# A two-layer graph network on one core: the first stage in another order, and one gather in eighty fetched row by row by SyncE

## The chip, the cores and the metric

The kernel runs on one core of a Trainium2 chip. The metric is the device time of one execution in microseconds (us). Nine runs of the kernel before gave a median of 4908.98 us (4884.85 to 4942.95).

## The reference, cut to what matters

12,500 nodes with 128 features, 200,000 edges sorted by their target `dst`. All numbers are float32.

```
h = relu(layernorm(x))
agg = segment_sum(h[src], dst)
x = x + agg @ W_rel.T + b_rel + h @ W_root.T          # layer 0

h = relu(layernorm(x))
ew = silu(edge_attr_50 @ We1 + be1) @ We2 + be2       # one row of 128 per edge
agg = segment_sum(h[src] * ew, dst)
x = x + h + (silu(agg @ Wn1 + bn1) @ Wn2 + bn2)       # layer 1
```

## The kernel before

**Tiles.** A tile is 128 edges, a group is 8 tiles (1024 edges); there are 196 groups in each layer, and the last has 3 tiles. Nodes are worked on in 25 batches of 512.

**One group.** `fetch` (L205) has GpSimd (POOL) issue one indirect DMA for each tile (L214): 128 rows of 128 floats are gathered from HBM into one of six buffers `hs`. The buffer of group k is free when the scatter of group k-6 is done (L208). `compare` (L223) builds on VectorE (DVE) a 0/1 matrix `oh` of 128 edges by a window of 128 targets for each tile. `scatter` (L328, matmul L336) multiplies the 8 gathered tiles with their `oh` on TensorE (PE) and sums them in one PSUM bank; `add` (L344, L353) adds that bank into `agg` in SBUF, at an offset that it loads into registers (L347).

**Layer 0** gathers rows of h. For the first 28 groups (FG = number of batches + FB, L110) h is not in HBM yet, so the raw x is gathered and normalised in SBUF by `norm` (L275), two half groups of 4 tiles each. Beside each of the first 25 groups `node_root` (L377) normalises one batch of nodes, stores h to HBM (`h0_d`), transposes it on PE (L396), copies the result on ScalarE (ACT, L405), and multiplies it with W_root after a matmul that lays the bias b_rel down (L407, L409); DVE then adds x and writes `keep` (L417). I call this stretch the first stage. `push` (L265) runs the first half of a unit at once and the second half with the next unit; `later` holds the steps after that. From group 28 on rows of `h0_d` are gathered, for which POOL waits until all batches are stored (L212). When all edges of a batch are summed, `node_sum`, `node_norm` and `node_keep` (L422 to L458) finish it: agg times W_rel (L429), layer norm, h stored to `h1_d` by SP.

**Layer 1** also has for each group g the edge weights. `hidden(g+2)` (L298) takes the edge features: for each pair of groups SP loads 400 KB into one of two buffers `ef` (`load`, L290, DMA L295; the buffer is free when `hidden` of the pair before the last is done, L294), PE multiplies with We1 (L306), ACT applies silu (L309). `weigh(g+1)` (L312) multiplies with We2 (L317); DVE adds the bias (L324) and multiplies the gathered rows in place (L326). When a batch is complete, `node_hidden` and `node_out` (L461, L470) compute its output, DVE adds `keep` (L483) and SP stores it (`out_x`, L370, after the wait at L485).

**Order.** Every engine works through its own instructions in the order in which the loop L590 to L615 emits them; a wait (`at`) holds all that stands behind it on that engine. Within one iteration g of layer 1 the order is: add(g-1), hidden(g+2), scatter(g), weigh(g+1), then the steps on nodes that `plan` (L568) put beside this group. So SP's list in layer 1 is made of `ef` loads, each two iterations ahead of its use, and of output stores, each of which waits for the newest result of DVE. A store falls into every eighth iteration or so: iterations 10, 18, 26, 34, 42, 50, then 59, 67, ... 139, then 146, 154, ... 186, and two at the end.

Of the kernel before, what the change touches and what calls it, by code (L numbers as in the profile page):

```python
# [11 lines left out]
I32 = mybir.dt.int32  # L12
# [6 lines left out]
P = 128  # L19
D = 128  # L20
# [7 lines left out]
OB = 3  # L28
EG = 2
XB = 4  # L30
FB = 3
EPS = 1e-5


# [31 lines left out]
    return need  # L66


@with_exitstack
def kernel(  # L70
    ctx: ExitStack,
# [1 line left out]
    n_edges: int,  # L73
    x: bass.AP,
    src_t: bass.AP,
    dst_t: bass.AP,
    ef_t: bass.AP,
    need: bass.AP,
# [42 lines left out]
    def single(shape, name, dtype=F32):  # L121
        return const.tile(shape, dtype, name=name)
# [3 lines left out]
    agg = single([P, NW * WG], "agg")  # L126
    keep = single([P, -(-N // P), D], "keep")
    src_sb = single([P, NT], "src_sb", I32)
    rel = single([P, NG, GT], "rel")
    base_i = single([1, NG], "base_i", I32)  # L130
    bad_i = single([1, 1], "bad_i", I32)
# [11 lines left out]
    with (  # L143
# [7 lines left out]
        inside_n, = many(1, [P, 1], "inside_n")  # L151
        total, = many(1, [1, 2], "total")
        hs = many(HB, [P, GT, D], "hs")
        oh = many(OB, [P, GT, W], "oh")
        ef = many(2, [P, EG * GE], "ef")
        dst_i = ef[1][:, :NT].bitcast(I32).rearrange("p (g t) -> p g t", t=GT)
# [48 lines left out]
        def fetch(layer, g):  # L205

            k = layer * NG + g
            at(G, done["src", 0 if g < 8 else 1], done.get(("ap", k - HB)))  # L208
            if layer:
                at(G, *(done["h1 out", b] for b in range(max(0, NBT - 2), NBT)))  # L210
            elif g >= FG:
                at(G, *(done["h0 out", b] for b in range(max(0, NBT - 3), NBT)))  # L212
            for t in range(tiles_of[g]):
                ins = G.indirect_dma_start(  # L214
                    out=hs[k % HB][:, t, :], out_offset=None,
                    in_=h1_d if layer else x if g < FG else h0_d,
                    in_offset=bass.IndirectOffsetOnAxis(
                        ap=src_sb[:, g * GT + t : g * GT + t + 1], axis=0
                    ),
                )  # L220
                done["hs", k] = inc(ins, f"hs{k % HB}", 16)

        def compare(layer, g):  # L223
            n = tiles_of[g]
# [87 lines left out]
        def weigh(g):  # L312

            n = tiles_of[g]
            at(T, done["hid", g], done.get(("msg", g - 1)), done["keep", NBT - 1])
            for t in range(n):
                ins = T.matmul(  # L317
                    wp[:, t, :], hid[g % 2][:, t * P : (t + 1) * P], we2_sb, start=True, stop=True
                )
            done["wp", g] = inc(ins, "pe")  # L320
            compare(1, g)
            at(V, done["wp", g])
            w, h = wp[:, :n, :], hs[(NG + g) % HB][:, :n, :]
            ins = V.tensor_add(w, w, be2_sb.unsqueeze(1).to_broadcast([P, n, D]))  # L324
            at(V, inc(ins, "dve"), done["hs", NG + g])
            done["msg", g] = inc(V.tensor_mul(h, w, h), "dve")  # L326

        def scatter(layer, g):  # L328
            k = layer * NG + g
            if layer:  # L330
                at(T, done["msg", g])
            else:
                at(T, done["h of", g] if g < FG else done["hs", k], done["oh", k])
            at(T, done.get(("add", k - AB)))
            for t in range(tiles_of[g]):
                ins = T.matmul(  # L336
                    ap[k % AB], hs[k % HB][:, t, :], oh[k % OB][:, t, :],
                    start=(t == 0), stop=(t == tiles_of[g] - 1),
                )
            done["ap", k] = inc(ins, "pe")  # L340

# [35 lines left out]
        def node_root(b):  # L377

            n0, nt = batches[b]
            xr, h, i = xt[b % XB], h0[b % 3], b % 2  # L380
            dev = []

            def first():
                dev.append(
                    stats(xr, nt, P, stn[i], mvn[i], sdn[i], (done["xt", b], done.get(("h0", b - 2))))
                )

            def second():
                at(A, scales(nt, P, mvn[i], sdn[i], rsn[i], nmn[i], *dev))
                at(A, done.get(("h0 out", b - 3)), done.get(("tp", b - 3)))  # L390
                done["h0", b] = normalized(h, xr, nt, P, rsn[i], nmn[i])
                at(S, done["h0", b])
                done["h0 out", b] = node_dma(b, h, h0_d, f"h0out{b % 3}", False)
                at(T, done["h0", b], done.get(("hT", b - 1)), done["ident"])
                for t in range(nt):
                    ins = T.transpose(tp[:, t, :], h[:, t, :], ident)  # L396
                done["tp", b] = inc(ins, "pe")
                later.append((clock[0] + 1, lambda: node_root_b(b)))

            return first, second  # L400

        def node_root_b(b):
            n0, nt = batches[b]
            at(A, done["tp", b], done.get(("rp", b - 1)))
            done["hT", b] = inc(A.copy(hT[0][:, :nt, :], tp[:, :nt, :]), "act")  # L405
            at(T, done["hT", b], done.get(("kept", b - 1)), done["const"], done["ones"])
            T.matmul(rp[:, :nt, :], ones_r, b_rel_r[:, :nt, :], start=True, stop=False)  # L407
            for t in range(nt):
                ins = T.matmul(rp[:, t, :], hT[0][:, t, :], w_root_sb, start=False, stop=(t == nt - 1))  # L409
            done["rp", b] = inc(ins, "pe")  # L410
            later.append((clock[0] + 1, lambda: node_root_c(b)))

        def node_root_c(b):
            n0, nt = batches[b]
            t0 = n0 // P
            at(V, done["rp", b])
            ins = V.tensor_add(keep[:, t0 : t0 + nt, :], rp[:, :nt, :], xt[b % XB][:, :nt, :])  # L417
            done["kept", b] = inc(ins, "dve")
            if b + XB < NBT:
                node_load(b + XB)  # L420

        def node_sum(b):  # L422

            n0, nt = batches[b]
            t0 = n0 // P
            at(T, done["add", ready[b]], done.get(("keep", b - 1)), done["const"])
            for t in range(nt):
                s = n0 + t * P
                ins = T.matmul(op[:, t, :], agg[:, s : s + P], w_rel_sb, start=True, stop=True)  # L429
            done["op", b] = inc(ins, "pe")  # L430
            at(V, done["op", b], done["kept", b])
            o = op[:, :nt, :]
            ins = V.tensor_add(o, o, keep[:, t0 : t0 + nt, :])  # L433
            done["dev", b] = stats(
                op, nt, P, stn[2], mvn[2], sdn[2], (inc(ins, "dve"), done.get(("h1", b - 1)))
            )
            ins = V.memset(agg[:, n0 : n0 + nt * P], 0.0)
            done["agg"] = inc(ins, "dve")
# [51 lines left out]
        with tc.tile_critical():  # L490
# [8 lines left out]
            for b in range(min(XB, NBT)):  # L499
                node_load(b)  # L500
            done["need"] = inc(S.dma_start(out=need_f, in_=need), "need", 16)
            for t, ap_ in (
                (w_root_sb, w_root_t), (b_rel_r, b_rel.unsqueeze(1).to_broadcast([1, NB, D])),
                (w_rel_sb, w_rel_t), (we1_sb, we1), (we2_sb, we2),
                (wn1_sb, wn1), (wn2_sb, wn2), (be1_sb, be1), (bn1_sb, bn1),
                (be2_sb, be2.to_broadcast([P, D])),
                (bn2_r, bn2.unsqueeze(1).to_broadcast([1, NB, D])),
            ):
                done["const"] = inc(S.dma_start(out=t, in_=ap_), "const", 16)
# [74 lines left out]
            for layer in range(2):  # L584
# [5 lines left out]
                for g in range(NG):  # L590
# [2 lines left out]
                        fetch(layer, g + 1)  # L593
                    if not layer:
                        if g + 1 < NG:
                            ins = compare(0, g + 1)
                        if g:
                            done["oh", k + 1] = add(0, g - 1)
                        elif g + 1 < NG:
                            done["oh", k + 1] = inc(ins, "dve")  # L600
                        if g < FG:
                            for c in range(-(-tiles_of[g] // NB)):
                                push(norm(g, c))
                            push(node_root(g) if g < NBT else nothing)
                        scatter(0, g)
                    else:
                        if g:
                            add(1, g - 1)
                        if g + 2 < NG:
                            hidden(g + 2)  # L610
                        scatter(1, g)
                        if g + 1 < NG:
                            weigh(g + 1)
                    for what in beside[layer].get(g, ()):
                        what()  # L615
                add(layer, NG - 1)
                for what in beside[layer].get(NG, ()):
                    what()
# [184 lines left out]
```

## Time and profile before

The profiled execution took 4917.91 us; its span, from the first to the last instruction, is 4916.0 us. It is 8.9 us above the median of the nine runs.

| stretch (us from the start) | what runs | POOL busy | PE busy | DVE busy | granted PE clock |
|---|---|---|---|---|---|
| 0 to 418 | layer 0, groups 0 to 27 (rows of x) | 236.74 | 213.37 | 173.73 | 0.65 |
| 418 to 2320 | layer 0, the other 168 groups | 1254.14 | 539.90 | 322.70 | 0.61 |
| 2320 to 4916 | layer 1, 196 groups | 1468.00 | 1465.10 | 756.29 | 0.74 |

How to read it: one indirect DMA of POOL is shown as 0.95 us (946 ns in the mean) and the next starts 0.30 us later when POOL waits for nothing, so a gather takes 1.25 us and a group of eight 10.0 us. The 0.30 us is not counted as busy. Groups in the table's stretches take (418 to 2320) 1902/168 = 11.3 us and (2320 to 4916) 2596/196 = 13.2 us each. In the lists below a row of the timeline is: start in us, length in us, engine and line, operation, written tile <- read tiles, count, and in brackets the idle time of the engine before it and what ended it. In a view of waits the columns are total us, times, longest us. "remote" and "another core or an unknown queue" stand for a wait whose end the profile can't attribute; "issue" for time in which the engine waited for nothing that the profile shows. SPq is SP issuing a DMA, not the transfer.

### The profile page before, as it was taken

How to read it: one execution, taken by the hardware profiler on the slowest of the kernel's cores; microseconds unless marked ns; L12 is line 12 of the kernel's file. 1: busy time of each engine (PE TensorE's matmuls, PEld its weight loads, DVE VectorE, ACT ScalarE, POOL GpSimd, SP SyncE). 2: the span in 40 equal slices, each digit the busy share in tenths (PEclk: the TensorE clock that was granted, in tenths of full speed). 3: DMA queues.
4: the chain of work that ended last, by engine and by line, in shares of the span. 5: the costliest groups of instructions: out<-in, count | busy, mean ns of one | idle time of the engine just before them, and what ended most of it. 6: DMA issues, size and time to landing. Idle time of an engine off the chain costs nothing.

```text
span 4916.0 us, 30563 instructions
## 1 busy us (share of the span) xinstructions
PE 2218.4 (45%) x11000; PEld 1786.3 (36%) x11000; DVE 1252.7 (25%) x2369; ACT 453.4 (9%) x778; POOL 2958.9 (60%) x3133
## 2 busy tenths in 40 slices
PE   3662332222322323224466556455445555556666
PEld 2442322222222223223344444343333343444444
DVE  2442211111111111112223233232222222333333
ACT  3441000000000000000001001010000000000101
POOL 6556666666666666665666566555544555566663
PEclk6666555655666666566677777777677777777777
DMA  3321211111111111112222222122222122222221
GB/s 85 82 71 47 54 48 50 50 48 50 49 49 50 49 48 52 49 49 55 59 58 66 58 63 63 52 54 54 52 57 53 52 55 54 57 58 60 70 66 43
DMA packets 159390, 274.89 MB, mean 56 GB/s; under 512 B 53231, under 2 KB 104058, under 8 KB 154330
## 3 DMA queue, kind: packets, MB, share of 16 engines
q0 software_dynamic: 100032, 205.07, 16.1%
q1 hardware_dynamic: 59002, 67.70, 5.0%
q8 instruction: 89, 1.46, 0.1%
q14 instruction: 71, 0.58, 0.0%
q10 hardware_dynamic: 196, 0.09, 0.0%
HBM read 253.44 MB, written 19.20 MB: 55 GB/s over the span
## 4 chain that ended last, share of the span: by engine, by line
another core or an unknown queue 45%; PE 23%; issue 15%; DVE 11%; DMA 2%; ACT 1%; DVEq 1%; POOL 0%; SPq 0%; POOLq 0%
PE bank L336 12%; PE pair L317 4%; DVE pair L324 3%; PE pair L306 3%; DVE oh L227 2%; DMA ef<-in_ef_t 2%; DVE hs L326 2%; DVE agg L353 1%; DVEq L347 1%; ACT h L257 1%; PE pair L407 1%; PE pair L409 1%; DVE st L238 1%; DVE stn L238 0%
## 5 line engine op out<-in xcount | busy, mean ns | idle before, releaser
L214 POOL DMA_INDIRECT hs<-h_d,src_sb x2902 | 2745.7, 946 | 1768.0 <-issue 838.0
L336 PE MATMUL bank<-oh,hs 128*128 128x128 f32 x6252 | 1164.2, 362 | 1893.5 <-issue 658.4
L336 PEld LDWEIGHTS bank<-oh,hs 128*128 128x128 f32 x6252 | 1088.9, 270 | 2093.4 <-issue 1385.4
L324 DVE TENSOR_TENSOR pair<-pair,be_sb 128x1024 f32<-128x1024 f32 x196 | 240.9, 1229 | 1746.2 <-remote 1029.5
L306 PE MATMUL pair<-ef,we_sb 50*128 50x512 f32 (+1 forms) x782 | 423.2, 661 | 283.9 <-DMA ef<-in_ef_t 251.6
L227 DVE TENSOR_TENSOR oh<-bank,rel 128x1024 f32<-128x1024 f32 x392 | 474.5, 1211 | 0.1
L317 PE MATMUL pair<-we_sb,hid 128*128 128x128 f32 x3126 | 443.3, 301 | 13.7 <-issue 6.7
L353 DVE TENSOR_TENSOR agg<-agg,bank 128x128 f32 x392 | 110.9, 283 | 1324.2 <-remote 1094.2
L317 PEld LDWEIGHTS pair<-we_sb,hid 128*128 128x128 f32 x3126 | 434.1, 221 | 13.2 <-issue 9.5
L309 ACT ACTIVATE hid<-pair,be_sb 128x1024 f32<-128x1024 f32 x196 | 217.8, 1111 | 2210.7 <-remote 1007.3
L306 PEld LDWEIGHTS pair<-ef,we_sb 50*128 50x128 f32 x782 | 139.6, 198 | 434.0 <-DMA ef<-in_ef_t 256.3
L214 POOL DMA_INDIRECT hs<-in_x,src_sb x224 | 212.0, 946 | 137.9 <-PE bank L336 66.4
L326 DVE TENSOR_TENSOR hs<-pair,hs 128x1024 f32<-128x1024 f32 x196 | 239.3, 1221 | 15.5 <-DMA hs<-h_d,src_sb 8.8
L429 PE MATMUL bank<-w_rel_sb,agg 128*128 128x128 f32 x196 | 45.7, 397 | 316.2 <-issue 200.4
L243 ACT ACTIVATE sdn<-mvn,eps 128x4 f32<-128x4 f32 (+1 forms) x50 | 14.8, 297 | 1764.4 <-DVE mvn L241 1384.8
L429 PEld LDWEIGHTS bank<-w_rel_sb,agg 128*128 128x128 f32 x196 | 39.4, 294 | 320.0 <-issue 202.7
L433 DVE TENSOR_TENSOR bank<-bank,keep 128x512 f32<-128x512 f32 (+1 forms) x25 | 17.2, 689 | 321.0 <-remote 248.8
L257 ACT ACTIVATE hs<-hs,nm,rs 128x128 f32<-128x128 f32 x224 | 91.5, 480 | 10.7 <-DVE nm L250 6.4
L396 PE MATMUL pair<-ident,h 128*128 128x128 f32 x98 | 26.1, 417 | 113.1 <-ACT h L257 82.4
L407 PE MATMUL pair<-b_rel_r,ones_r 1*128 1x512 f32 (+1 forms) x50 | 50.9, 1119 | 35.8 <-issue 29.4
L396 PEld LDWEIGHTS pair<-ident,h 128*128 128x128 f32 x98 | 16.3, 204 | 119.3 <-ACT h L257 88.0
L409 PEld LDWEIGHTS pair<-w_root_sb,hT 128*128 128x128 f32 x196 | 43.7, 327 | 36.8 <-issue 36.8
(57 smaller groups left out, 565.9 us busy)
## 6 DMA issues: line engine op xcount, KB each, us to landing
hs<-h_d,src_sb POOLq DMA_INDIRECT x2902
ef<-in_ef_t SPq DMA_DIRECT2D x98, 400.0 KB
h_d<-h SPq DMA_DIRECT2D x48, 256.0 KB
xt<-in_x SPq DMA_DIRECT2D x24, 256.0 KB
out_x<-xt SPq DMA_DIRECT2D x24, 256.0 KB
hs<-in_x,src_sb POOLq DMA_INDIRECT x224
ef<-in_dst_t SPq DMA_DIRECT2D x1, 784.0 KB, 4.5
src_sb<-in_src_t SPq DMA_DIRECT2D x1, 752.0 KB, 6.0
```

What stands on the lines that cost most here:

```text
L214: ins = G.indirect_dma_start(out=hs[k % HB][:, t, :], out_offset=None, in_=h1_d if layer else x if g < FG else h0_d, in_offset=bass.Indire ...
L227: return V.tensor_tensor(oh[k % OB][:, :n, :], io.unsqueeze(1).to_broadcast([P, n, W]), rel[:, g, :n].unsqueeze(2).to_broadcast([P, n, W]) ...
L257: ins = A.activation(h[:rows, t, :], xr[:rows, t, :], AF.Relu, bias=nm_[:rows, t : t + 1], scale=rs_[:rows, t : t + 1],)
L306: ins = T.matmul(hp_b[:, c : c + m], we1_sb, e[:, c : c + m], start=True, stop=True)
L309: ins = A.activation(hid[g % 2][:, :n], hp_b[:, :n], AF.Silu, bias=be1_sb)
L317: ins = T.matmul(wp[:, t, :], hid[g % 2][:, t * P : (t + 1) * P], we2_sb, start=True, stop=True)
L324: ins = V.tensor_add(w, w, be2_sb.unsqueeze(1).to_broadcast([P, n, D]))
L326: done["msg", g] = inc(V.tensor_mul(h, w, h), "dve")
L336: ins = T.matmul(ap[k % AB], hs[k % HB][:, t, :], oh[k % OB][:, t, :], start=(t == 0), stop=(t == tiles_of[g] - 1),)
L353: done["add", k] = inc(V.tensor_add(window, window, ap[k % AB]), "dve")
L407: T.matmul(rp[:, :nt, :], ones_r, b_rel_r[:, :nt, :], start=True, stop=False)
L409: ins = T.matmul(rp[:, t, :], hT[0][:, t, :], w_root_sb, start=False, stop=(t == nt - 1))
```

## The change

It has three parts.

1. In the first stage `compare` and the normalising units come before `add`, which moves to just ahead of `scatter`; `node_root` is cut into four steps instead of three, with two units between transpose and copy and two between the root matmuls and `keep`. The bias matmul of b_rel leaves this stage and goes into `node_sum`, ahead of its wait for `add`.
2. FB goes from 3 to 4, so that 29 groups are gathered from x.
3. For 35 groups (16 in layer 0: 40, 50, ... 190; 19 in layer 1: 11, 21, ... 191) POOL gathers only the first 7 tiles. The rows of the eighth are fetched by SP, one DMA of 512 bytes for each row, into a buffer `hx` (two of them). `rows(layer, g)` is emitted at the end of every iteration, behind the steps on nodes: it loads 12 or 16 of the 128 row numbers from SBUF into SP's registers in one instruction, and then issues one register instruction and one DMA for each row. Ten iterations fill one tile, which is used two iterations later. In all these are 4480 row DMAs, and SP's list grows by some 9,300 instructions. `scatter` waits for `hx` ahead of its last tile, and in layer 1 DVE multiplies the last tile apart.

```diff
-FB = 3
+FB = 4
+RG = 10
...
+def rows_apart(n_nodes, n_edges):
+    full = n_edges // GE
+    tiles = []
+    for layer in range(2):
+        begin = 0 if layer else -(-n_nodes // (NB * P)) + FB
+        while begin + RG + 1 < full:
+            tiles.append((layer, begin + RG + 1, begin))
+            begin += RG
+    return tiles
...
-            for t in range(tiles_of[g]):
+            for t in range(tiles_of[g] - ((layer, g) in place)):
                 ins = G.indirect_dma_start(
...
+        def rows(layer, g):
+            for i, (l, at_g, begin) in enumerate(apart):
+                if l != layer or not begin <= g < begin + RG:
+                    continue
+                lo, hi = (P // 4 * (g - begin + j) // RG * 4 for j in range(2))
+                if g == begin:
+                    at(S, done["rows"], done["ap", apart[i - 2][0] * NG + apart[i - 2][1]] if i > 1 else None)
...
+                _, nodes = nc.values_load_multi_w_load_instructions(
+                    row_sb[i : i + 1, lo:hi], engines=[mybir.EngineType.SP], min_val=0, max_val=N - 1,
...
+                for p, node in zip(range(lo, hi), nodes):
+                    ins = S.dma_start(
+                        out=hx[i % 2][p : p + 1, :], in_=(h1_d if layer else h0_d)[ds(node, 1), :]
+                    )
+                    done["hx", i] = inc(ins, f"hx{i % 4}", 16)
...
-            done["msg", g] = inc(V.tensor_mul(h, w, h), "dve")
+            i = place.get((1, g))
+            if i is not None:
+                V.tensor_mul(h[:, : n - 1, :], w[:, : n - 1, :], h[:, : n - 1, :])
+                at(V, done["hx", i])
+                ins = V.tensor_mul(hx[i % 2], w[:, n - 1, :], hx[i % 2])
...
-                later.append((clock[0] + 1, lambda: node_root_b(b)))
+                later.append((clock[0] + 2, lambda: node_root_b(b)))
...
-            T.matmul(rp[:, :nt, :], ones_r, b_rel_r[:, :nt, :], start=True, stop=False)
             for t in range(nt):
-                ins = T.matmul(rp[:, t, :], hT[0][:, t, :], w_root_sb, start=False, stop=(t == nt - 1))
+                ins = T.matmul(rp[:, t, :], hT[0][:, t, :], w_root_sb, start=True, stop=True)
             done["rp", b] = inc(ins, "pe")
-            later.append((clock[0] + 1, lambda: node_root_c(b)))
-
-        def node_root_c(b):
+            later.append((clock[0] + 2, lambda: node_root_d(b)))
...
-            at(T, done["add", ready[b]], done.get(("keep", b - 1)), done["const"])
+            at(T, done.get(("keep", b - 1)), done["const"], done["ones"])
+            T.matmul(op[:, :nt, :], ones_r, b_rel_r[:, :nt, :], start=True, stop=False)
+            at(T, done["add", ready[b]])
...
                         if g + 1 < NG:
-                            ins = compare(0, g + 1)
-                        if g:
-                            done["oh", k + 1] = add(0, g - 1)
-                        elif g + 1 < NG:
-                            done["oh", k + 1] = inc(ins, "dve")
+                            compared = compare(0, g + 1)
+                            if not g:
+                                done["oh", 1] = inc(compared, "dve")
                         if g < FG:
                             for c in range(-(-tiles_of[g] // NB)):
                                 push(norm(g, c))
                             push(node_root(g) if g < NBT else nothing)
+                        if g:
+                            done["oh", k + 1] = add(0, g - 1)
                         scatter(0, g)
...
                     for what in beside[layer].get(g, ()):
                         what()
+                    rows(layer, g)
```

## The prediction

> **What bounds the kernel now.** I read in this order: busy shares, costliest groups, waits by stage, then the timeline around one output store in layer 1, and SP's rows of issue durations. From the page's costliest groups:
>
> ```profile
> L214 POOL DMA_INDIRECT hs<-h_d,src_sb x2902 | 2745.7, 946 | 1768.0 <-issue 838.0
> L306 PE MATMUL pair<-ef,we_sb 50*128 50x512 f32 (+1 forms) x782 | 423.2, 661 | 283.9 <-DMA ef<-in_ef_t 251.6
> ```
>
> A gather is 946 ns, and most of POOL's "issue" idle is 0.30 us between two gathers: 1.25 us each, 10.0 us a group. Layer 0 after the first stage takes 1902/168 = 11.3 us a group, so POOL is nearly the bound there. Layer 1 takes 13.2: something else holds POOL for some 3 us a group. The waits of layer 1 (2320 to 4916) say what:
>
> ```profile
> POOL hs L214 <- PE bank L336: 541.1, 74, 18.3
> PE pair L306 <- DMA ef<-in_ef_t: 250.1, 22, 21.1
> ```
>
> POOL waits for scatters (its buffers are all full), and PE's `hidden` waits 22 times, 11.4 us each, for an `ef` load. There are 22 to 24 output stores. The timeline at one of them:
>
> ```profile
> 3111.33 0.68 DVE L483 TENSOR_TENSOR xt<-bank,keep 128x512 f32<-128x512 f32 x1
> 3112.04 0.41 SPq L370 DMA_DIRECT2D out_x<-xt  x1
> 3112.49 0.86 SPq L295 DMA_DIRECT2D ef<-in_ef_t  x2
> ...
> 3117.55 3.78 PE L306 MATMUL pair<-ef,we_sb 50*128 50x512 f32 x4 [19.12 <-DMA ef<-in_ef_t]
> 3121.26 3.78 PE L336 MATMUL bank<-oh,hs 128*128 128x128 f32 x16
> ...
> 3125.31 0.94 POOL L214 DMA_INDIRECT hs<-h_d,src_sb  x1 [17.96 <-PE bank L336]
> ```
>
> The reader sees a chain: the store waits on DVE, the `ef` load stands behind the store in SP's list, PE waits for the load, the scatter stands behind `hidden` on PE, POOL waits for the scatter. From store to `hidden` it is 5.5 us; at the other stores I read it is 5.1 to 7.1. At this point nothing covers a later `ef` load: its delay is paid in full.
>
> The first stage has its own pace. Gathers of successive groups start at 147.85, 160.72, 173.97, 187.27: 13.2 us a group. Its waits (100 to 350):
>
> ```profile
> DVE keep L417 <- PE pair L409: 87.2, 17, 5.1
> POOL hs L214 <- PE bank L336: 61.8, 19, 3.6
> ```
>
> DVE stands 5.1 us at L417 for the root matmuls of that same iteration, compares and adds stand behind it, and POOL waits some 3 us a group. At its end:
>
> ```profile
> 387.12 0.95 POOL L214 DMA_INDIRECT hs<-h_d,src_sb  x1 [34.99 <-DMA h_d<-h]
> ```
>
> **First stage in the other order.** `keep` now comes two units after the root matmuls, the copy two after the transpose, and the bias matmul (2.07 us a batch, L407) no longer stands ahead of the scatter. That removes the 5.1 us wait. What is late next is POOL itself: I take layer 0's pace, 11.3, for some 21 groups: 21 × (13.2 − 11.3) = −40. The 35 us wait is for the last h store; the batches end earlier by the same pace but POOL arrives earlier too, and the 29th group from x adds 11 us of work ahead of it; I take −15. Together **−55**. Ends: 0 (DVE's and ACT's lists are as long as before, so another wait may replace this one), and −102 (21 × the 3.2 us above the gathers' 10.0, and all 35). The bias matmul in `node_sum` is ahead of that step's wait for `add`; PE idles 316.2 us ahead of L429 in 25 batches, so it costs nothing; uncovered it would be 25 × 1.2 = 30.
>
> **One gather less in 35 groups.** 35 × 1.25 = **−44**; the end is 0, where POOL was not last. DVE's split multiply in layer 1 is one more instruction of about 0.28 us (L353 takes 283 ns for 128x128), and the larger one shrinks by about 0.13: 19 × 0.15 = **+3**.
>
> **Rows by SP.** 128 rows a tile, over ten iterations: ten loads of registers, 128 register instructions, 128 DMA issues, all on SP's queue. The trace has no one-row DMA from an address in a register on SP. The nearest rows (min/median/max ns, then first and last start):
>
> ```profile
> L295 SPq DMA_DIRECT2D ef<-in_ef_t x98: 281/282/462, 2244.5 to 4856.3; - x98
> L370 SPq DMA_DIRECT2D h_d<-h x51: 332/365/421, 48.1 to 2303.6; - x51
> L509 SPq DMA_DIRECT2D b_rel_r<-in_b_rel x1: 736/736/736, 8.2 to 8.2; - x1
> L501 SPq DMA_DIRECT2D need_f<-in_need x1: 2056/2056/2056, 5.6 to 5.6; - x1
> L347 DVEq FUSED_REGOPS  x392: 183/186/206, 23.5 to 4891.2; - x196
> L347 DVEq TENSOR_LOAD <-base_i x98: 339/343/602, 22.9 to 4889.9; - x98
> ```
>
> The register instruction is 0.186 on DVE's queue, with gaps of some 0.04 to 0.05 around it. The DMA is bounded below by 0.28 (50 rows) and above by 2.06 (one row, need_f, right behind four large loads at the start); b_rel_r, four rows, took 0.74. Most issues, and all those in steady running, are 0.28 to 0.41, so I take 0.37: 0.19 + 0.04 + 0.37 + 0.05 = **0.65 us a row**. Ends 0.33 (issue and gap alone) and 2.3. The load of 12 or 16 values I take at 0.40, near the 0.34 of four values (up to 4 × 0.34 = 1.37). A tile is 128 × 0.65 + 10 × 0.4 = 87 us of SP; ten groups are 113 us in layer 0 and 132 in layer 1. So SP keeps up, `hx` is there in time, and the waits for it cost 0. SP becomes the bound above 0.85 us a row in layer 0, and 1.0 in layer 1.
>
> The Trainium skill speaks against the 0.37 ("DMA: Bandwidth & Descriptors", "Why a DMA increments its semaphore by 16 and not by 1"): a transfer of fewer than 16 pieces uses fewer engines, and the issuing sequencer itself writes the semaphore increments of the engines not used. A one-row DMA would thus have 15 of them; the rows of 0.74 (four) and 2.06 (one) beside 0.28 fit that order. The page has no time for it; by 2.06 the sum would be the last rival's. The same page ("Latency and other measured facts") puts a `tensor_load` at 600 ns at least; this trace shows 343, and by 600 the 35 loads priced below would add 9 us.
>
> **What stands behind the rows.** `rows(g)` is at the end of every iteration, so whatever SP issues next stands behind it: in layer 0 the h stores and in layer 1 the output stores and the `ef` loads. In layer 0 the store of h1 has slack. In layer 1 an `ef` load without a store ahead of it is issued two iterations before its use, and 8 to 9 us of rows per group fit into that. But after an output store, which waits for DVE far along in the group, the rows now stand between the store and the `ef` load that PE waits for. From SP's list in the changed kernel: 12 stores in even iterations (10 to 50 and 146 to 186) have 24 to 28 rows and two loads of registers ahead of the next `ef` load, 304 rows and 24 loads in all; 11 stores in odd ones (59 to 139) have 12 to 16 rows and one load: 144 rows and 11 loads. So 448 × 0.65 + 35 × 0.40 = 291 + 14 = **+305**. Low end: 448 × 0.33 + 35 × 0.34 = 160; and 0, if something covers it. What could cover it is an `ef` buffer ahead or PE working on something else; the timeline shows PE idle 19 us at that point, and POOL out of buffers.
>
> **Sum.** −55 − 44 + 3 + 305 = +209. On the profiled execution's own 4917.9 that is 5127; this execution lies 8.9 above the median, so against the runs' median 5118, rounded to **5120**.
>
> **Rivals.**
>
> *Gains fail, stalls come.* First stage and gathers give nothing (an engine other than POOL is last in both): 4909 + 308 = 5217. For it: "remote" waits in the trace show that other engines progress poorly while POOL issues in long bursts (in layer 1, `DVE pair L324 <- remote: 1029.5, 89, 16.7`). I count it within the forecast's own range, 5020 to 5240, with it **0.50**.
>
> *Half the stall is taken up* (POOL refills its six buffers, and the pair after a store runs at 10 us a group where the mean is 13.2): 4909 − 96 + 155 = 4968; 4935 to 5020, **0.12**.
>
> *Faster.* One mechanism: the `ef` load is not late. The place is SP's list behind the 23 output stores; the price is 448 rows, against a gain of 96 − 5 = 91 us. It decides when a row costs under 91/448 = 0.2 us there, or when the wait for the store moves so that PE reaches `hidden` later than the load anyway. Then 4909 − 91 = 4818. Against it: even an issue alone has not been under 0.28, and PE waits for `ef` in 22 of 23 cases. For it: the register instruction could run beside the issue. **0.17**.
>
> *No change.* Stalls of some 90 us eat the gains exactly; 4885 to 4935, about 4910, **0.08**.
>
> *SP becomes the bound.* The one-row issue costs 0.74, so a row 0.74 + 0.19 + 0.09 = 1.02, a tile 132 to 135 us: layer 0 then loses 16 × (132 − 113) = +304, `ef` 448 × 1.02 + 14 = +471, gains −95: about 5590. At 2.3 us a row 4480 × 2.3 alone is over 10,000. For it: the two smallest transfers have the longest issues. Against it: both stood at the start behind other issues. **0.13**.
>
> **How the numbers follow.** About 0.5% (25 us) is what a measurement of this kernel can tell. Slower by more: 0.50 + 0.12 + 0.13 = 0.75. Faster 0.17, same 0.08. The range goes from the faster case's 4820 to 5420, leaving out most of SP as the bound and half of the faster case: 4820 to 5420. The likeliest case alone is 5020 to 5240.
>
> **What the profile after would show.** The row DMAs on SP near 0.37 us; from output store to `hidden` some 14 us (odd stores) and 22 us (even ones) instead of 5.5; PE waiting for `ef` some 550 us in all instead of 250, and POOL's waits for L336 up by about the same; the first stage at some 11.3 us a group and the 35 us wait shorter; no wait of PE for `hx`. It would be wrong if a row costs over 0.85 us (waits for `hx` on PE and DVE), or if waits for `ef` don't grow, or if the first stage keeps 13 us.

## The result and the profile after

The changed kernel took 5640.53 us (median of 10 runs, 5618.43 to 5660.88), the kernel before beside it 4912.02 (31 runs): ratio 1.1481, interval 1.1452 to 1.1509. The profiled execution took 5631.3 us, its span is 5629.4. Ratios leave out runs far above the others of their kernel: one in experiment 4 (6941.4 us) and one in experiment 5 (4858.81 us).

That holds on one kind of chip. The experiments fell on several chips, and these are of two kinds: on some the kernel before takes 4862 to 4961 us, on others 3996 to 4004, and there the changed kernel is faster, 3895.67 us, ratio 0.9746 (0.9729 to 0.9762). I call them the first and the second kind. The prediction and the result above are of the first kind. A ratio is always to the kernel before on the same chip.

**Where the 713 us of the two profiled executions lie** (5631.3 − 4917.9), by the starts of gathers that open a stretch:

| stretch | before | after | difference |
|---|---|---|---|
| to the first gather of group 29 | 397.13 | 354.27 | −42.9 |
| from there to the first gather of layer 1 (2306.34; 2732.71) | 1909.2 | 2378.4 | +469.2 |
| from there to the end | 2611.6 | 2898.6 | +287.0 |

The chain that ended last, in the kernel before and then in after, and from the page of after its costliest groups (busy us, mean ns | idle before, and what ended most of it):

```profile
another core or an unknown queue 45%; PE 23%; issue 15%; DVE 11%; DMA 2%; ACT 1%; DVEq 1%; POOL 0%; SPq 0%; POOLq 0%
```
```profile
SPq 28%; issue 26%; another core or an unknown queue 19%; PE 16%; DVE 8%; DMA 2%; ACT 1%; DVEq 0%; POOL 0%
...
L231 POOL DMA_INDIRECT hs<-h_d,src_sb x2859 | 2705.8, 946 | 2536.7 <-PE bank L388 1286.4
...
L347 PE MATMUL pair<-ef,we_sb 50*128 50x512 f32 (+1 forms) x782 | 435.6, 681 | 569.0 <-DMA ef<-in_ef_t 567.8
...
L388 PE MATMUL bank<-oh,hx 128*128 128x128 f32 x70 | 21.7, 406 | 753.5 <-DMA hx<-h_d 753.5
```

SP, which held 0% of the chain before, holds 28% of it now. PE waits 753.5 us for `hx`, in 15 waits of some 50 us: these are 15 of the 16 tiles of layer 0. Its wait for `ef` has grown from 251.6 to 567.8, of which 67.0 is one wait at the end of layer 0. POOL idles mostly for scatters now, no longer by its own pace.

The first stage (waits from 100 to 335, where those of the kernel before were from 100 to 350, and POOL's timeline at its end):

```profile
DVE keep L472 <- remote: 46.3, 5, 11.1
...
DVE keep L472 <- PE pair L464: 4.3, 4, 2.1
```
```profile
354.27 0.94 POOL L231 DMA_INDIRECT hs<-h_d,src_sb  x1 [18.31 <-PE pair L464]
```

DVE's wait at `keep` for the root matmuls is 4.3 us instead of 87.2. The wait at `keep` has not gone with it: 46.3 us of it now end by nothing that the profile can name, and in all DVE waits 64.9 us there instead of 97.5. POOL waits 18.3 us at the end instead of 35.0. Groups 20 to 27 start 11.5 us apart, (326.25 − 233.86)/8; the same groups of the kernel before start 12.9 apart. (The 13.2 of the prediction comes from four starts, and these give 13.1.) Of the 42.9 us the pace gives 26 and the shorter wait 17.

An output store in layer 1 (timeline; of before the store at 3112.04 was shown):

```profile
3049.78 0.42 SPq L422 DMA_DIRECT2D out_x<-xt  x1
...
3051.93 18.53 SPq L259 DMA_DIRECT2D hx<-h_d  x28
...
3070.51 0.29 SPq L336 DMA_DIRECT2D ef<-in_ef_t  x1
...
3075.21 3.77 PE L347 MATMUL pair<-ef,we_sb 50*128 50x512 f32 x4 [16.66 <-DMA ef<-in_ef_t]
```

28 rows stand between store and load, as the prediction counted, and `hidden` comes 25.4 us after the store instead of 5.5. Over all 23 stores it is 25.3 us in the mean at the 12 with 24 to 28 rows and 12.8 at the 11 with 12 to 16, against 6.1 in the kernel before.

SP's row instructions in after (min/median/max ns, first and last start), then the same of the changed kernel on a chip of the second kind:

```profile
L259 SPq FUSED_REGOPS  x4480: 1/37/1396, 354.6 to 5566.6; - x195
L259 SPq MOVE hx<-h_d x4480: 1/29/1396, 354.7 to 5566.7; - x195
L259 SPq DMA_DIRECT2D hx<-h_d x4480: 1/227/1398, 355.1 to 5567.0; - x195
```
```profile
L259 SPq FUSED_REGOPS  x4480: 37/37/56, 269.7 to 3831.2; - x195
L259 SPq MOVE hx<-h_d x4480: 29/29/38, 269.8 to 3831.3; - x195
L259 SPq DMA_DIRECT2D hx<-h_d x4480: 224/228/312, 270.3 to 3831.4; - x195
L254 SPq TENSOR_LOAD <-row_sb x350: 931/1034/1797, 268.7 to 3823.8; - x175
```

A row is three instructions, not two. On the second kind they take 37, 29 and 228 ns, and a row comes every 0.41 us. In after the same instructions take up to 1.4 us each, the register instruction too, whose row names no tile. When this happens is seen on SP's queue, beside POOL's gathers:

```profile
355.14 18.20 SPq L259 DMA_DIRECT2D hx<-h_d  x12
...
553.38 19.02 SPq L259 DMA_DIRECT2D hx<-h_d  x40
...
573.40 0.79 PE L388 MATMUL bank<-oh,hx 128*128 128x128 f32 x2 [40.90 <-DMA hx<-h_d]
...
574.46 0.95 POOL L231 DMA_INDIRECT hs<-h_d,src_sb  x1 [24.48 <-PE bank L388]
```

From 355 on POOL gathers without a pause: 12 rows in 18.2 us. From 553.4 to 572.4 POOL stands still (a wait of 24.48 us for a scatter, until 574.46): 40 rows in 19.0 us, with their loads of registers. All loads and rows of a tile take 140 us in the mean in layer 0 (2243 us in 16 tiles), where ten groups took 114 in the kernel before (10 × 1909.2/167; the 11.3 us a group and the 113 ahead of the result come from a stretch whose bounds lie some groups late). On the second kind of chip a tile takes 65 (2278/35).

### The profile page after: what moved, and what is told of

Same layout as the page of the kernel before. It is cut to its first block, busy times and chain, and to the rows that moved or that the text cites. A ratio compares the mean times of both kernels' runs of the same rounds, so it can differ in the third digit from the quotient of the medians.

```text
span 5629.4 us, 44372 instructions
## 1 busy us (share of the span) xinstructions
PE 2208.5 (39%) x11000; PEld 1792.0 (32%) x11000; DVE 1254.1 (22%) x2408; ACT 460.3 (8%) x788; POOL 2926.6 (52%) x3098
## 3 DMA queue, kind: packets, MB, share of 16 engines
q1 hardware_dynamic: 68004, 70.03, 4.5%
## 4 chain that ended last, share of the span: by engine, by line
SPq 28%; issue 26%; another core or an unknown queue 19%; PE 16%; DVE 8%; DMA 2%; ACT 1%; DVEq 0%; POOL 0%
SPq L259 24%; PE bank L388 7%; PE pair L347 4%; PE pair L358 4%; SPq L254 3%; DVE pair L365 3%; DMA ef<-in_ef_t 2%; DVE oh L268 2%; DVE hs L373 1%; DVE st L279 1%; DVE agg L405 0%; ACT hs L298 0%; DVE stn L279 0%; ACT h L298 0%
## 5 line engine op out<-in xcount | busy, mean ns | idle before, releaser
L231 POOL DMA_INDIRECT hs<-h_d,src_sb x2859 | 2705.8, 946 | 2536.7 <-PE bank L388 1286.4
L347 PE MATMUL pair<-ef,we_sb 50*128 50x512 f32 (+1 forms) x782 | 435.6, 681 | 569.0 <-DMA ef<-in_ef_t 567.8
L388 PE MATMUL bank<-oh,hx 128*128 128x128 f32 x70 | 21.7, 406 | 753.5 <-DMA hx<-h_d 753.5
L388 PEld LDWEIGHTS bank<-oh,hx 128*128 128x128 f32 x70 | 15.9, 281 | 757.3 <-DMA hx<-h_d 757.3
L373 DVE TENSOR_TENSOR hs<-pair,hs 128x1024 f32<-128x1024 f32 x177 | 216.1, 1221 | 14.7 <-DMA hs<-h_d,src_sb 8.6
L279 DVE BATCH_NORM_STATS2 st<-hs 128x6 f32<-128x128 f32 x232 | 50.1, 278 | 4.5 <-DMA hs<-in_x,src_sb 4.1
```

Source lines behind the costliest of these rows:

```text
L231: ins = G.indirect_dma_start(out=hs[k % HB][:, t, :], out_offset=None, in_=h1_d if layer else x if g < FG else h0_d, in_offset=bass.Indire ...
L279: ins = V.bn_stats(st_[:rows, t, :], xr[:rows, t, :])
L347: ins = T.matmul(hp_b[:, c : c + m], we1_sb, e[:, c : c + m], start=True, stop=True)
L373: ins = V.tensor_mul(h, w, h)
L388: ins = T.matmul(ap[k % AB], hx[i % 2] if last and i is not None else hs[k % HB][:, t, :], oh[k % OB][:, t, :], start=(t == 0), stop=last,)
```

## The experiments

**Theory** after the result: SP becomes the bound in layer 0 since each of its instructions is slow while POOL gathers; in layer 1 the `ef` loads are late behind the rows, as predicted. **Rivals**: the new first stage costs later on; the row DMA itself is slow; only the wait for `hx` costs; the rows themselves bound layer 1. The 489 and 267 us in some expectations come from a boundary of the layers that I had placed 16 gathers too late; by the table above they are 469 and 287.

**1. The first stage alone.**

```diff
-    for layer in range(2):
-        begin = 0 if layer else -(-n_nodes // (NB * P)) + FB
+    for layer in ():
+        begin = 0
```

> The first stage in its new order and FB = 4, no rows on SP and all eight gathers by POOL. If the first stage is a gain by itself (in the changed kernel the gathers of group 29 start at 354.3 us, before at 397.1): 43 us, 4912 - 43 = about 4870. Rival: the time won in the first stage is lost again behind it (POOL waits for scatters or stores there): no change, 4912.

Measured (first kind): 4907.3, before 4960.65, ratio 0.9914 (0.9878 to 0.9951): 43 us less by the ratio, 24 to 61 by its interval (the medians lie 53 apart). The gain of the first stage is real, and is not lost behind it.

**2. The rows with the old first stage** (FB = 3, the first stage's part of the change undone).

> The rows on SP with the first stage and FB as before. If the parts add up, the changed kernel's 5640 + 43 = about 5683. Rival: the new order of the first stage is part of the loss (the bias matmul in node_sum delays layer 0): well below 5640.

Measured: 5697.38, ratio 1.1529 (1.1451 to 1.1607), against 1.1481 of the full change. The rows lose all of it by themselves, and the new first stage is no part of the loss. The 43 us of the first stage are too small to be seen between these two ratios.

**3. and 4. Rows in one layer.**

```diff
-    for layer in range(2):
+    for layer in (0,):      # in the other kernel (1,)
```

> The new first stage, and rows by SP in layer 0 alone (16 tiles). Theory: SP is the bound in layer 0, since its instructions are slow while POOL gathers; from the traces layer 0 behind group 29 is 489 us longer, so 4870 + 489 = about 5360. The prediction's step (SP keeps up, only gathers saved): 4870 - 20 = 4850.

> The new first stage, and rows by SP in layer 1 alone (19 tiles). Theory (late ef loads behind the rows, as predicted at +305 - 24 + 3): layer 1 of the changed kernel is 267 us longer by the traces, so 4870 + 267 = about 5137, PE's wait for ef near 570 us instead of 250. Rival: layer 1 only pays for what layer 0 left behind on SP: below 5000.

Measured: layer 0 alone 5366.52, ratio 1.0856 (1.0782 to 1.0930); layer 1 alone 5194.4, ratio 1.0501 (1.0415 to 1.0587). Over the first stage alone that is 459 and 287 us, each known to some 40 us; by the stretches of the profiled executions it is 472 in layer 0 and 253 in layer 1. So these are two separate losses, each of about the size that the table of the stretches gives. The waits from 2733 to the end, with rows in layer 1 and then without:

```profile
PE pair L347 <- DMA ef<-in_ef_t: 431.9, 20, 28.3
PE bank L388 <- DVE hs L373: 430.3, 53, 15.9
...
PE bank L388 <- DVE hx L371: 107.0, 11, 15.9
```
```profile
PE bank L388 <- DVE hs L373: 582.5, 74, 14.8
...
PE pair L347 <- DMA ef<-in_ef_t: 239.8, 19, 20.8
```

Layer 1 begins near 2265 in both kernels, so these rows leave out its first 468 us. Over all of layer 1 PE waits 497.9 us for `ef` with rows and 247.5 without: +250, where layer 1 is 253 longer. POOL's waits for scatters there grow beside it by 227, from 603.3 to 830.1. The wait for DVE's multiply of the tile from SP (107 us, 11 times) is no second loss: it stands where PE waited for the multiply of `hs`, and the two together fall from 582.5 to 537.3.

**5. Row addresses known beforehand**: one instruction a row instead of three, and no loads of registers. The eighth tiles then hold other rows than the reference's.

```diff
-                _, nodes = nc.values_load_multi_w_load_instructions(...)
-                for p, node in zip(range(lo, hi), nodes):
+                for p in range(lo, hi):
+                    node = (i * 331 + p * 97) % N
```

> The changed kernel with row addresses known beforehand (rows p*97 + i*331 in place of the sources, so the eighth tiles hold other rows than the reference's): one DMA instruction a row, no register instructions and no loads of registers. Theory (every instruction of SP pays while POOL gathers): a row costs a third, some 0.5 us instead of 1.0 in the mean, a tile some 64 us, SP is no longer the bound in layer 0 (no waits for hx), layer 1 keeps a third to a half of its 267: 4870 - 44 + 110 = about 4950, at most 5050. Rival (the row DMA itself is what is slow beside the gathers): a row stays above 0.85 us, over 5400.

> The kernel with row addresses known beforehand again (the eighth tiles hold other rows than the reference's): one SP instruction a row. Where the kernel before takes some 4950 us. Theory (every instruction of SP pays while POOL gathers): a row costs a third, SP is no longer the bound in layer 0, 4870 - 44 + 110 = about 4950, at most 5050, ratio near 1.00. Rival (the row DMA itself is what is slow): a row stays above 0.85 us, over 5400, ratio over 1.09. Where the kernel before takes 3996: 3894 again.

> Row addresses known beforehand (the eighth tiles hold other rows than the reference's): one SP instruction a row. Where the kernel before takes some 4950 us. Theory (every instruction of SP pays while POOL gathers): ratio near 1.00, at most 1.03. Rival (the row DMA itself is what is slow): ratio over 1.09. Where it takes 3996: 0.974 again.

Three times on the second kind of chip: 3894.17, 3894.86 and 3896.66, ratio 0.974 to 0.975, as the changed kernel itself there. This does not tell the theories apart, since rows cost nothing there. In layer 0 alone it then ran on a chip of the first kind:

> The new first stage, and in layer 0 alone rows with addresses known beforehand (the eighth tiles there hold other rows than the reference's): one SP instruction a row. Where the kernel before takes some 4950 us. Theory (every instruction of SP pays while POOL gathers): SP is not the bound, ratio 0.99 to 1.01 instead of 1.086. Rival (the row DMA is what is slow): over 1.05. Where it takes 3996: 3996 - 59 - 20 = 3917.

Measured (first kind, before 4861.61): 4802.29, ratio 0.9884 (0.9844 to 0.9924), where three instructions a row and the loads gave 1.0856. As many DMAs of the same size are there, and the loss is gone. Its rows:

```profile
L256 SPq DMA_DIRECT2D hx<-h_d x2048: 2/253/1401, 352.1 to 2215.6; - x187
```

Single issues still reach 1.4 us, as in after; but there is one a row, and PE's waits for `hx` are 16.6 us in all instead of 787 with rows by three instructions in layer 0 alone. So the row DMA alone is not what bounds SP; the number of instructions that SP has to bring through POOL's gathers is. The loads of registers went with the others, but the traces give their share. By the time from the start of each of SP's instructions to the start of the next, within each group of rows, the 16 tiles of layer 0 in after and on the second kind spend: register instructions 609 and 156 us, moves 613 and 130, DMAs 824 and 532, loads 158 and 187. The loads are no slower; the growth of 1200 us is in the three instructions of a row, and over three quarters of it is in the two that the fixed addresses leave out. This kernel and that of experiment 3 ran on different chips of the first kind; that the delay is there on both is shown by the steps in the last section.

**6. Rows fetched and not used**: POOL gathers all eight tiles, the scatter and DVE use these.

```diff
-            for t in range(tiles_of[g] - ((layer, g) in place)):
+            for t in range(tiles_of[g]):
...
-                    ap[k % AB], hx[i % 2] if last and i is not None else hs[k % HB][:, t, :],
+                    ap[k % AB], hs[k % HB][:, t, :],
```

> The changed kernel, but POOL gathers all eight tiles and the scatter and DVE use these: SP still fetches every row, and nobody waits for hx. Theory (SP's list is too long for layer 0 and holds the h1 stores back; POOL, never stopped by hx, leaves SP even slower): the waits for hx are replaced by waits for the stores of h1, layer 0 still loses 350 us or more, in all 5500 to 5800. Rival (only the waits for hx cost in layer 0, the rows run alongside): layer 0 as in the kernel with the new first stage alone, layer 1 some 267 longer, about 5140.

> Rows fetched by SP, all eight tiles gathered by POOL, nobody waits for hx. Where the kernel before takes some 4950 us. Theory (SP's list is too long for layer 0 and holds the h1 stores back): 5500 to 5800. Rival (only the waits for hx cost in layer 0): about 5140. Where the kernel before takes 3996: 3937 again.

Second kind both times: 3937.5 (0.9853) and 3938.24 (0.9851, 0.9834 to 0.9867). The first stage alone on this kind:

> The new first stage alone, without rows, eight gathers. Where the kernel before takes some 4950 us: ratio 0.991 again. Where it takes 3996: 3996 - 58 = 3938, as with the rows fetched and unused, if the rows cost nothing there; below 3930 if they cost something.

Measured: 3936.6, before 3997.2, ratio 0.9844 (0.9828 to 0.9861). Beside 3938.24: 4480 row DMAs and 350 loads cost nothing on this kind of chip. What the expectation for the first kind said stays untried, and with it the rival that only the waits for `hx` cost there.

**7. Seven gathers, and one DMA of 128 neighbouring rows a tile.**

```diff
-                    ins = S.dma_start(out=hx[i % 2][p : p + 1, :], in_=(...)[ds(node, 1), :])
+                    ins = S.dma_start(out=hx[i % 2], in_=(...)[i * P : (i + 1) * P, :])   # once a tile
```

The eighth tiles hold other rows than the reference's here too.

> The new first stage, seven gathers in the 35 groups, and instead of the row DMAs one DMA of 128 neighbouring rows for each tile (so the eighth tiles hold other rows than the reference's). Prices the saved gathers alone: 4870 - 44 = about 4826 if POOL is last in all 35 groups, 4870 if in none; layer 0 alone would give 20.

Measured (second kind): 3894.39, ratio 0.9746 (0.9732 to 0.9759). Against 3937.5 with eight gathers (experiment 6, the same chip): 43 us for 35 gathers, 1.23 each.

**8. The ef loads issued by ACT.**

```diff
-            at(S, done.get(("hp", g - EG - 1)), done["inside"])
-            ins = S.dma_start(out=e[:EF, : n * GE], ...)
+            at(A, done.get(("hp", g - EG - 1)), done["inside"])
+            ins = A.dma_start(out=e[:EF, : n * GE], ...)
```

> The changed kernel with the ef loads issued by ACT instead of SP, so that neither output stores nor rows stand ahead of them. Theory (layer 1 loses by late ef loads): PE's waits for ef go, layer 1 gives back its 267 or more: 5640 - 290 = about 5350; layer 0 as it was. Rival (SP's rows bound layer 1 themselves, and waits of DVE for hx take their place): above 5550.

> The changed kernel with the ef loads issued by ACT. Where the kernel before takes some 4950 us. Theory (layer 1 loses by late ef loads): 5640 - 290 = about 5350, ratio 1.09. Rival (SP's rows bound layer 1 themselves): above 5550, ratio over 1.12. Where the kernel before takes 3996: 3894 again.

> The ef loads issued by ACT. Where the kernel before takes some 4950 us. Theory (layer 1 loses by late ef loads): ratio 1.09. Rival (SP's rows bound layer 1 themselves): over 1.12. Where it takes 3996: 0.974 again.

With rows in layer 1 alone:

> The new first stage, rows by SP in layer 1 alone, and the ef loads issued by ACT. Where the kernel before takes some 4950 us. Theory (layer 1 loses by ef loads that stand behind the rows): the loss goes, ratio 0.99 or less (with SP's list the ratio was 1.050, without rows 0.991). Rival (the rows themselves bound layer 1, or ACT's list holds the loads up as long): 1.03 or more. Where the kernel before takes 3996: POOL is last, and 19 gathers of 1.25 us are saved on top of the first stage's 59: 3996 - 59 - 24 = 3913.

> The new first stage, rows by SP in layer 1 alone, and the ef loads issued by ACT. Where the kernel before takes some 4900 us. Theory (layer 1 loses by ef loads that stand behind the rows): ratio 0.99 or less. Rival (the rows themselves bound layer 1, or ACT's list holds the loads up as long): 1.03 or more. Where the kernel before takes 3996: 0.979 again.

All five fell on the second kind: 3894.19, 3895.15 and 3894.95 (ratio 0.974 to 0.975); 3921.8 and 3914.21 (0.9791 and 0.9796). So on the first kind this edit was never measured, and the path of layer 1's loss stands on the traces alone.

**9. The changed kernel on the second kind of chip.**

> The changed kernel unaltered, beside the others of this call and the kernel before. Where the kernel before takes some 4950 us: 5640 again (ratio 1.148), with row instructions of SP slowed while POOL gathers. Where it takes some 3996, as in the call with the ef loads on ACT: SP's rows cost 0.41 us there also while POOL gathers, POOL is last throughout, and only the gains are left: 3996 - 58 (first stage) - 44 (35 gathers of 1.25) = about 3894. Rival: the late ef loads cost there too, about 3894 + 50 or more.

Measured: 3895.67, ratio 0.9746 (0.9729 to 0.9762). Its chain, and two of its waits:

```profile
POOL 64%; issue 22%; PE 7%; DMA 3%; DVE 2%; SPq 2%; DVEq 0%; ACT 0%; POOLq 0%
```
```profile
PE pair L347 <- DMA ef<-in_ef_t: 349.6, 24, 17.1
POOL hs L231 <- PE bank L388: 1.5, 5, 0.3
```

PE waits 349.6 us for `ef` here too, against 150.8 with the first stage alone: from store to `hidden` it is 11.8 to 20.1 us. But POOL waits 1.5 us for scatters in all. It is last throughout (0.30 us "issue" between its gathers and nothing else), its six buffers never run out, and so the rival that the late loads cost something here fell. Experiment 7, with no rows ahead of the loads, takes as long (3894.39).

## Why the prediction was wrong

It gave 5120 (4820 to 5420); measured was 5640.53. The sign was right and the size wrong. Its steps in order:

| step | predicted | first kind | second kind |
|---|---|---|---|
| first stage | −55 | −43 (trace and experiment 1) | −61 (3997.2 − 3936.6) |
| 35 gathers | −44 | not separable | −43 (3938.24 − 3895.67) |
| `ef` loads behind rows | +305 | +304 by the distances from store to `hidden`: 12 × (25.3 − 6.1) + 11 × (12.8 − 6.1); +250 by PE's waits for `ef` (experiment 4) | 0 |
| layer 1 in all | +284 | +287 (253 by the profiled executions of experiment 4) | −24 (by the traces of the first stage alone and of the changed kernel) |
| waits for `hx` ("SP keeps up, `hx` is there in time, and the waits for it cost 0") | 0 | +469 with gathers saved, all in layer 0 | 0 |

**The step that failed** is the last: the price of a row on SP, and with it "SP keeps up". I put a row at 0.65 us and a tile at 87; in layer 0 a row took 1.02, (2243 − 158)/2048, and a tile 140. By the sums in experiment 5 a row is a register instruction of 0.30 us, a move of 0.30, which stood in no term, and a DMA of 0.44; a load of registers took 0.99 and not 0.40. The tile's 140 us compare with 114 for the same ten groups in the kernel before. 2243 − 16 × 114.3 = 414, and the last store of h at the end of layer 0, also behind the rows, made POOL wait 68.9 us instead of 20.0: +49. That is 463, measured 469; the 16 gathers saved there count for nothing in this reckoning, since POOL was not last. The prediction's own sign of being wrong, over 0.85 us a row and waits for `hx`, is what came. The rival "SP becomes the bound" had the right step and the right price (1.02 us a row), by luck, from the wrong reason: it put the cost on the one-row DMA. Its ground was misread too: `be_sb` and `bn_sb`, 0.5 KB each, are smaller than `need_f` and `b_rel_r`, and their issues took 0.43 us. On the second kind the one-row DMA is 228 ns, the shortest DMA issue on SP. The cost is that three instructions a row have to come through POOL's bursts. For the ring that forms, the timeline around 553 above is the picture: SP falls behind while POOL gathers, PE waits for `hx`, POOL's buffers fill and it stops, and only then SP runs at 0.41 us a row and completes the tile.

**It could have been seen.** The prediction itself quoted the trace's "remote" waits (1029.5 us of DVE at L324) as a sign that other engines progress poorly while POOL issues in long bursts. I let that speak against the gains and did not apply it to 9,300 new instructions on SP, though a queue of many short instructions has the most to lose by a delay for each. The durations of the nearest rows came from stretches, or from queues, in which this did not show.

**The `ef` step** was right in place, count and price: the 448 rows and 35 loads were predicted from SP's list, and of the delay of 304 us PE's waits show 250 on the first kind of chip. That its price of 0.65 a row came out was luck, an accident of two errors: undisturbed rows are cheaper (0.41), those under gathers dearer. That the delay is the cause of layer 1's loss is read from the traces, not shown by removing it on the first kind.

**The bias matmul and the split multiply** left no mark that the runs can tell; neither was tried alone.

The Trainium skill ("DMA: Bandwidth & Descriptors", "Why a DMA increments its semaphore by 16 and not by 1") has the issuing sequencer write what unused engines do not post; the trace has two packets for each row DMA (68,004 on that queue in after, 59,002 before, for 4480 rows), which fits one engine a row. If these writes take time on SP, the runs put a bound on it, since a one-row issue of 228 ns on the second kind is below the 292 of a 50-row one in the same trace. The same page's floor of some 600 ns for a `tensor_load` ("Latency and other measured facts") agrees with the 1034 ns of 12 to 16 values and not with the 343 ns that four values took on DVE's queue.

**What stays open**: what makes the first kind of chip slow SP, and what the two kinds are. That SP's delay comes from POOL's gathers, and not from the transfers that they start, is read from the timing alone; no run changes the gathers on the first kind. The mean granted PE clock differs between the kinds too, 0.687 and 0.715 with the first stage alone, and no run varies it by itself. On the first kind the first stage alone takes 4907.3, on the second 3936.6. DVE's largest wait in both traces:

```profile
DVE pair L365 <- remote: 1201.7, 93, 50.2
```
```profile
DVE pair L365 <- PE pair L358: 814.2, 196, 16.1
```

On the second kind each of the 196 waits ends with the matmul that DVE waits for. On the first, the profile finds no event that ends 93 of them: the matmul was recorded earlier. One such place of the kernel before: the last matmul of L317 ends at 3161.4, DVE's L324 starts at 3173.13, and POOL's burst of gathers has ended at 3172.9. So a delay beside POOL's bursts is older than the change and lies in the kernel before too. I read it as the larger part of the 971 us between the kinds, since a gather takes the same on both; no run here shows that.

## What to carry to other kernels

Price work that moves to an idle queue in instructions, not in transfers, and take the duration of each from a stretch in which the other engines do what they will do beside it. A prefetch at the end of an iteration stands ahead of everything that its queue issues next: count, from the list in order, what stands between each wait and the next load that an engine needs. And a gain or loss off the longest engine is worth nothing: the late loads went with some 250 us of loss where POOL ran out of buffers, and with none where it did not.

## What the runs showed of the hardware

On the first kind of chip SP's step from one row instruction to the next grows with the time for which POOL has gathered without a pause (mean of all steps under 6 us on L259, from the traces):

| POOL's burst so far | after | changed kernel, second kind |
|---|---|---|
| POOL idle for over 4 us | 0.17 us | no such pause after the first groups |
| under 3 us | 0.20 | |
| 5 to 10 us | 0.44 | |
| 10 to 15 us | 0.71 | |
| 15 to 20 us | 0.98 | |
| over 20 us | 1.36 | 0.17 |

Many of the long steps are 0.70 us or 1.40. In bursts over 15 us the step after a register instruction is 1.12 us in the mean, after a move 1.10 and after a DMA 1.19, so it goes by the instruction and not by what it is. With one instruction a row (experiment 5, another chip of the first kind) the step in bursts over 20 us is 1.32, and with three in layer 0 alone (experiment 3) it is 1.37. POOL's gathers themselves are 946 ns in after and 944 on the second kind: the engine beside whose bursts the delay appears does not show it. And the runs of the kernel before on one chip of the second kind agree within 0.1 to 0.3% (3995.84 to 4000.18, 3996.14 to 4008.45), those of the result on the first kind only within 1.6% (4876.99 to 4955.87).
